# Attention over four images: x of images 1 to 3 loaded in 128-byte pieces and transposed on VectorE, and the halves of a group's output added by an accumulating DMA

## The chip, the cores and the metric

The kernel runs on one core of one Trainium2 chip. A core has five engines, each with its own instruction queue: TensorE (PE: matrix products; PEld is its weight load), VectorE (DVE), ScalarE (ACT), GpSimd (POOL) and SyncE (SP). DMAs are issued from the queues of SP, ACT and POOL and are moved by 16 DMA engines. SBUF is the working memory of 128 partitions, and PSUM the eight banks into which TensorE writes. The metric is device time in microseconds (us) of one execution.

## The reference

x has shape (4, 64, 64, 256): four images of N = 4096 positions with C = 256 channels. The reference computes, for each image,

```python
q = jnp.einsum('bwhc,cd->bwhd', x, Wq) + bq      # 128 channels
k = jnp.einsum('bwhc,cd->bwhd', x, Wk) + bk      # 128 channels
v = jnp.einsum('bwhc,cd->bwhd', x, Wv) + bv      # 256 channels
pq, pk, pv = q.reshape(B, -1, N), k.reshape(B, -1, N), v.reshape(B, -1, N)
energy = jnp.einsum('bcn,bcm->bnm', pq, pk)
attention = jax.nn.softmax(energy, axis=-1)      # 4096 x 4096 for each image
out = jnp.einsum('bcm,bnm->bcn', pv, attention)
return gamma * out.reshape(B, W, H, C) + x
```

All is float32. The reshape does not transpose: it only cuts the same memory into other rows.

## The kernel before, in words

**Precision.** A float32 operand is written as a sum of parts in the faster fp32r type: an upper part h, which ACT makes, and two rests l and d, which DVE makes from h and the operand. A product is then three matmuls. The three parts have the numbers 0, 1 and 2, and part 2 (d) goes into a matmul of its own.

**The main loop.** It runs over n = 0 to 511 (line 693): four images of 128 steps. An image has NG = 8 groups of 512 output columns; a group has NU = 16 steps, t = 0 to 15, and each step takes 256 of the 4096 rows of k. Step n issues, in this order:
- `cross(n + 2)`: the part-2 product of q and k, two matmuls, scaled on ACT (L368, L369);
- `attend(n, 0)`: six matmuls of the exponentials with half of v into the accumulators a0 and b0 (L442);
- `energy(n + 2)`: the other four matmuls of q and k (L383) and two exponentials on ACT (L386);
- `load_k`: a DMA of 384 KB on POOL's queue for step n + 5, into one of three buffers (L355);
- `store()`: stores of finished projections, on SP's queue (L338);
- `upper(n + 2)`: h on ACT (L392);
- `halves(n + 1)` on DVE: the running row sum (L403), l (L418) and d (L420);
- `attend(n, 1)`: six matmuls into a1 and b1;
- `proceed()`: one piece of every group that is being finished.

At t = 15 ACT empties a0 and b0 (L462) into a tile o, in the place of `upper`, and at t = 0 of the next group DVE empties a1 and b1 (L460) into the same tile. The tile o has one buffer, so the first of these waits for the output store of the group before.

**Finishing a group.** `finish` is a generator that advances by one piece with each step. In terms of t of the following group: at t = 15 and 0 the row sums go to DRAM and come back in another layout (zd, two stores; y, eight loads, all on SP's queue); at t = 3 DVE adds the two halves of o (L479); at t = 6 DVE reduces and transposes y and takes the reciprocal (L482 to L490), and SP stores it (L491); at t = 7 SP loads it, spread over all partitions, into a part of the second half of o (L494); at t = 9 DVE multiplies (L497); at t = 10 a DMA on POOL's queue adds x to o in place (L501); at t = 13 SP stores the group's output, 512 KB (L504).

**Projections.** Those of image 0 are made ahead of the loop. Those of images 1 to 3 are made beside the attention of the image before, in `step(p, engine)`: a pair of chunks of x takes R = 16 steps, r = 0 to 15, and from n = 18 on r = t - 1. One group so carries one pair, and images 1 to 3 have 24 pairs. In the order of r:
- r = 0: PE transposes both chunks, eight 128x128 transposes into two PSUM banks (L219);
- r = 1, 2: ACT makes h of each chunk (L155); r = 1 to 4: DVE makes d and l, one operation in each step (L165);
- r = 5, 6: PE multiplies by Wq and Wk (L257), and DVE adds the bias at r = 5 (L285);
- r = 7 to 10: forms of q and k (L307, L310); r = 9 to 12: PE makes v (L274); r = 11 to 14: forms of v;
- r = 12: SP loads the next pair of x, two DMAs of 256 KB (L211), once PE has used up the buffer.

The raw x of a pair and the d of that pair share one buffer (tag "xd", bufs=1).

**The order of the work.** The order on each engine is the order written out here. A scheduler adds the waits: each instruction waits for its inputs and for the release of the buffer that it writes. The DMAs of SP's queue start in order and take eight completion semaphores in turn, and each of them waits until the one eight before it has landed. In image 4 (n from 384 on) there are no projections.

Of the kernel before, what the change touches and what calls it, by code (L numbers as in the profile page):

```python
# [13 lines left out]
ALU = mybir.AluOpType  # L14
# [6 lines left out]
def kernel(  # L21
# [36 lines left out]
    nc = tc.nc  # L58
# [5 lines left out]
    KC = C // P  # L64
# [5 lines left out]
    def columns(t, nb):  # L70
        return t.rearrange("b w h c -> b (w h c)").rearrange(
            "b (a s g f) -> b g a s f", a=P, s=2, f=nb
        )

    XB = 256
    xv = columns(x, XB)
# [24 lines left out]
    with ExitStack() as fast:  # L101
# [43 lines left out]
        qd, kf, vf, units, loads, now = {}, {}, {}, {}, {}, {}  # L145
# [42 lines left out]
        def bank(name, shape, b, ring):  # L188
            if b:
                tile_ = spare(name, shape)  # L190
                now["turn"] += 1
                return tile_
            pool, tag = next(rings[ring])
            return pool.tile(shape, F32, tag=tag, name=name)

        def spare(name, shape):
            pool, tag = now["banks"][now["turn"] % len(now["banks"])]
            return pool.tile(shape, F32, tag=tag, name=name)

        def load_x(b, i):  # L200
            if b == B or i >= NI:
                return
            if b == 0:
                t = xs4[:, i % 4]
                if i:
                    nc.sync.dma_start(t, xv[b, i])
                loads["x", b, i] = t
                return
            pair = work.tile([P, 2, 2, XB], F32, tag="xd", name=f"x_{b}_{i}", bufs=1)
            for u in range(2):  # L210
                nc.sync.dma_start(pair[:, u], xv[b, i + u])  # L211
                loads["x", b, i + u] = pair[:, u]

        def transposed(b, i):
            xs = loads.pop(("x", b, i))
            tp = units["xt", b, i] = bank(f"xt_{b}_{i}", [P, KC, 2, P], b, 0)
            for k in range(KC):
                for s in range(2):
                    nc.tensor.transpose(tp[:, k, s, :], xs[:, s, k * P : (k + 1) * P], ident)  # L219

        def x_forms(b, i):

            y = units.pop(("xt", b, i))
            if b == 0:
                if i % 3 < 2:
                    f = ppool.tile([P, 3, KC, 2, P], F32R, tag="ld", name=f"xf_{b}_{i}")
                else:
                    f = work.tile([P, 4, KC, 2, P], F32R, tag="xf", name=f"xf_{b}_{i}", bufs=1)
                f = [f[:, j] for j in range(3)]
            else:  # L230
                if i % 2 == 0:
                    shape = [P, 2, KC, 2, 2, P]
                    f = work.tile(shape, F32R, tag="xf", name=f"xf_{b}_{i}", bufs=1)
                    d = work.tile([P, *shape[2:]], F32R, tag="xd", name=f"xd_{b}_{i}", bufs=1)
                    now["xf"] = [f[:, 0], f[:, 1], d]
                f = [y_[:, :, i % 2] for y_ in now["xf"]]
            units["xf", b, i] = f
            yield from split(*f, y, b == 0 and i > 1)
# [44 lines left out]
        def seed_qk(b, i):  # L283
            y = units[0, b, i]
            nc.vector.scalar_tensor_tensor(  # L285
                y, y, REST, bias.unsqueeze(1).to_broadcast([P, 2, C]), ALU.mult, ALU.add
            )
# [8 lines left out]
        def seed_v_pair(b, i, eh):  # L296
            y = units["v", b, i, eh]
            nc.scalar.activation(y, y, AF.Identity, bias=bvs[:, eh : eh + 1], scale=REST)
# [45 lines left out]
        def q_tile(g, name, dtype=F32R):  # L344
            return work.tile([P, NJ, 3, P], dtype, tag=f"q{g % 2}", name=name, bufs=1)
# [118 lines left out]
        def finish(n, o, s):  # L464
            b, g = divmod(n, NG)
            r4 = rall[:, n, :]
            for i in range(2):
                nc.sync.dma_start(zd[n, i], s[:, i, :])
            yield
            y = q_tile(n, f"y_{n}", F32).rearrange("p j f a -> p (j f) a")  # L470
            for j in range(NJ):
                for i in range(2):
                    nc.sync.dma_start(
                        y[j * 32 : (j + 1) * 32, NJ * i : NJ * (i + 1)],
                        zd[n, i].rearrange("(a p) (j c) -> j p a c", p=32, j=NJ)[j],
                    )
            for _ in range(3):
                yield
            nc.vector.tensor_tensor(o[:, 0], o[:, 0], o[:, 1], ALU.add)  # L479
            for _ in range(3):  # L480
                yield
            nc.vector.tensor_reduce(  # L482
                y[:, 8].rearrange("p (f c) -> p c f", f=NJ),
                y[:, :8].rearrange("p a (c f) -> p c f a", f=NJ),
                AX.X,
                ALU.add,
            )
            nc.vector.transpose(y[:, 9], y[:, 8])
            nc.vector.tensor_reduce(r4, y[:, 9].rearrange("p (f c) -> p f c", f=NJ), AX.X, ALU.add)
            nc.vector.reciprocal(r4, r4)  # L490
            nc.sync.dma_start(rd[n, :].rearrange("(p j) -> p j", j=NJ), r4)  # L491
            yield
            r = o[:, 1, 0]
            nc.sync.dma_start(r, rd[n, :].partition_broadcast(P))  # L494
            yield
            yield
            nc.vector.tensor_tensor(  # L497
                o[:, 0], o[:, 0], r.unsqueeze(1).to_broadcast([P, 2, NB]), ALU.mult
            )
            yield  # L500
            nc.gpsimd.dma_start(o[:, 0], xg[b, g], accum_op=ALU.add)  # L501
            for _ in range(3):
                yield
            nc.sync.dma_start(og[b, g], o[:, 0])  # L504
# [50 lines left out]
        def step(n, engine):  # L555

            if n < 0:
                return
            b, u = divmod(n, STEPS)
            i, r = divmod(u, R)  # L560
            b, i = b + 1, 2 * i
            if b >= B:
                return
            made = now["made"]

            def begin(key, pieces):
                made[key] = pieces
                next(pieces)

            if engine == "pe":  # L570
                if r == 0:
                    transposed(b, i)
                    transposed(b, i + 1)
                elif r == 5:
                    products(b, i, 0, (2,))
                    products(b, i + 1, 0, (2,))
                elif r == 6:
                    products(b, i, 0, (0, 1))
                    products(b, i + 1, 0, (0, 1))
                elif r in (9, 11):  # L580
                    products_v(b, i, r // 11, (2,))
                elif r in (10, 12):
                    products_v(b, i, r // 12, (0, 1))
            elif engine == "act":
                if r in (1, 2):
                    begin(("x", r - 1), x_forms(b, i + r - 1))
                elif r in (7, 8):
                    begin(("qk", r - 7), qk_forms(b, i + r - 7))
                elif r in (10, 12):
                    seed_v_pair(b, i, r // 12)  # L590
                    if r == 12:
                        load_x(b + (i + 2) // NI, (i + 2) % NI)
                elif r in (11, 13):
                    begin(("v", r // 13), v_pair_forms(b, i, r // 13))
            else:
                if 1 <= r <= 4:
                    next(made["x", (r - 1) // 2])
                elif r == 5:
                    seed_qk(b, i)
                    seed_qk(b, i + 1)  # L600
                elif 7 <= r <= 10:
                    next(made["qk", (r - 7) // 2])
                    if r % 2 == 0:
                        next(made["qk", (r - 7) // 2], None)
                elif 11 <= r <= 14:
                    next(made["v", (r - 11) // 2])
                    if r % 2 == 0:
                        next(made["v", (r - 11) // 2], None)
# [84 lines left out]
        for n in range(B * STEPS):  # L693
            b, u = divmod(n, STEPS)
# [14 lines left out]
            p = n - 2 + (n > 17)  # L709
# [32 lines left out]
            for m in range(2 * NU):  # L742
                c, r = divmod(n + NU - 3 - 13 * m // 16, STEPS)
# [8 lines left out]
    with tc.If(nc.values_load(again[0:1, 0:1]) > 0), ExitStack() as general:  # L752
# [91 lines left out]
        for b in range(B):  # L844
# [16 lines left out]
            for g in range(NG):  # L861
                ps = []
                mx = work.tile([P, 2, NB], F32, tag="mx", name=f"gmx_{b}_{g}")
                for t in range(NP):
# [9 lines left out]
                    p = ppool.tile([P, 2, NB], F32, tag="p", name=f"gp_{b}_{g}_{t}")  # L874
# [6 lines left out]
                tp = ps_t.tile([P, NJ, P], F32, tag="t", name=f"gmt_{b}_{g}")  # L881
# [45 lines left out]
                r = work.tile([P, NB], F32, tag="r", name=f"gr_{b}_{g}")  # L927
# [36 lines left out]
```

## Time and profile before

| | us |
|---|---|
| median of three runs | 2321.32 (2320.11 to 2322.51) |
| the profiled execution | 2319.64 |
| its span, first to last instruction | 2317.9 |
| PE busy | 2307.0 |
| DVE busy | 2174.3 |
| ACT busy | 1796.9 |
| POOL busy | 417.1 |
| granted TensorE clock | 0.999 |

A row of the profile names the line of the kernel, the engine and the operation, then output<-inputs, the shapes, and the count; after a bar the busy time in us and the mean ns of one, and after a second bar the engine's idle time just ahead of these instructions and what ended it. A row of the timeline begins with the start and the duration in us. A row of the waits has the total in us, the count and the longest. A row of DMA issues has the count, the size of one and the median us from issue to landing. Matmuls overlap in the trace, so what PE needs is read from the distance between starts, not from durations.

### The profile page before, as it was taken

Reading aid. Unit: us, or ns where it says so; the run is one execution under the profiler, and the core shown is the slowest. Engines: PE = TensorE matmul, PEld = TensorE weight load, DVE = VectorE, ACT = ScalarE, POOL = GpSimd, SP = SyncE. Lnnn points to the kernel's source line nnn. Section 1 sums busy time; section 2 is a strip of 40 time slices with the busy share of each in tenths; the row PEclk is TensorE's granted clock in tenths of the full one; section 3 lists DMA queues with packets and bytes.
Section 4 is the critical chain, followed back from the end, with each engine's and each line's share of the span. In section 5 each row is a group of like instructions: output and inputs, shape, how many; then the busy total and the mean of one; then the engine's idle time right before and its main releaser. Section 6 shows DMA issues by size and latency. Waiting matters only on the chain.

```text
span 2317.9 us, 31970 instructions
## 1 busy us (share of the span) xinstructions
PE 2307.0 (100%) x10758; PEld 1931.5 (83%) x10758; DVE 2174.3 (94%) x2174; ACT 1796.9 (78%) x2917; POOL 417.1 (18%) x716
## 2 busy tenths in 40 slices
PE   9999999999999999999999999999999999999998
PEld 9888888888888888888888888888888888888887
DVE  8999999999999999999999999999999999888988
ACT  7778777787777777777777777777787777888775
POOL 7111111111221111111122111111112211111110
PEclk9999999999999999999999999999999999999999
DMA  8557765577896776666799667755679855455553
GB/s 273 162 168 207 206 176 154 170 204 205 266 268 184 208 207 179 166 170 194 201 292 267 186 182 207 199 167 165 173 223 289 258 140 141 141 136 149 154 150 97
DMA packets 232190, 445.30 MB, mean 192 GB/s; under 512 B 27986, under 2 KB 109652, under 8 KB 232020
## 3 DMA queue, kind: packets, MB, share of 16 engines
q0 software_dynamic: 101120, 280.54, 45.5%
q1 hardware_dynamic: 130352, 162.38, 20.6%
q8 instruction: 88, 1.44, 0.3%
q14 instruction: 82, 0.67, 0.1%
q10 hardware_dynamic: 548, 0.26, 0.0%
HBM read 321.92 MB, written 120.39 MB: 191 GB/s over the span
## 4 chain that ended last, share of the span: by engine, by line
PE 99%; DVE 0%; ACT 0%; DMA 0%; issue 0%; ACTq 0%; DVEq 0%
PE a L442 40%; PE e L383 20%; PE b L442 20%; PE e L368 10%; PE qv L257 5%; PE v L274 3%; PE xt L219 1%; DMA raw<-in_L_conv_Wk_dram 0%; ACT qv L292 0%; DVE xf L165 0%; PE zp L517 0%; DVE o_last L547 0%; DVE o_last L542 0%; DVE qv L285 0%; DVE o_last L548 0%
## 5 line engine op out<-in xcount | busy, mean ns | idle before, releaser
L386 ACT ACTIVATE x<-e 128x512 f32<-128x512 f32 x960 | 522.4, 596 | 323.6 <-PE e L383 323.5
L369 ACT ACTIVATE e<-e 128x512 f32<-128x512 f32 x1024 | 546.7, 571 | 132.2 <-PE e L368 132.2
L442 PE MATMUL a<-h,v 128*128 128x512 f32 x2048 | 633.5, 390 | 0.0
L442 PE MATMUL a<-ld,v 128*128 128x512 f32 x2048 | 630.9, 389 | 0.0
L442 PE MATMUL b<-ld,v 128*128 128x512 f32 x2048 | 630.8, 389 | 0.0
L418 DVE TENSOR_TENSOR ld<-x,h 128x1024 fp32r<-128x1024 f32 x480 | 584.6, 1218 | 35.1 <-ACT h L392 22.3
L403 DVE TENSOR_TENSOR s<-s,x 128x1024 f32<-128x1024 f32 x480 | 584.2, 1217 | 33.9 <-ACT x L386 32.6
L355 POOL DMA_DIRECT2D k<-kf x512 | 272.5, 532 | 1845.7 <-PE e L383 1745.2
L420 DVE SCALAR_TENSOR_TENSOR ld<-h,x 128x1024 fp32r<-128x1024 f32 x480 | 584.0, 1217 | 0.0
L383 PE MATMUL e<-q,k 128*128 128x512 f32 x2048 | 547.7, 389 | 0.0
L392 ACT ACTIVATE h<-x 128x1024 fp32r<-128x1024 f32 x480 | 510.5, 1064 | 14.3
L442 PEld LDWEIGHTS a<-ld,v 128*128 128x128 f32 x2048 | 384.4, 188 | 80.6
L442 PEld LDWEIGHTS b<-ld,v 128*128 128x128 f32 x2048 | 384.3, 188 | 80.3 <-DVE ld L420 0.2
L383 PEld LDWEIGHTS e<-q,k 128*128 128x128 f32 x2048 | 384.2, 188 | 79.7
L442 PEld LDWEIGHTS a<-h,v 128*128 128x128 f32 x2048 | 379.6, 188 | 74.2
L368 PE MATMUL e<-q,k 128*128 128x512 f32 x1024 | 315.5, 389 | 0.0
L368 PEld LDWEIGHTS e<-q,k 128*128 128x128 f32 x1024 | 191.9, 188 | 39.8
L310 DVE SCALAR_TENSOR_TENSOR f<-f,qv 128x512 fp32r<-128x512 f32 x128 | 85.5, 678 | 0.3
L418 DVE TENSOR_TENSOR ld<-s,h 128x1024 fp32r<-128x1024 f32 x32 | 39.2, 1226 | 46.8 <-ACT h L392 46.8
L257 PE MATMUL qv<-wf,xf 128*128 128x256 f32 x576 | 77.2, 285 | 0.9 <-DVE qv L285 0.4
L257 PEld LDWEIGHTS qv<-wf,xf 128*128 128x128 f32 x576 | 73.7, 191 | 4.1 <-DVE xf L165 0.8
L165 DVE SCALAR_TENSOR_TENSOR vf<-vf,v 128x512 fp32r<-128x512 f32 x96 | 65.2, 679 | 0.0
(88 smaller groups left out, 1126.8 us busy)
## 6 DMA issues: line engine op xcount, KB each, us to landing
k<-kf POOLq DMA_DIRECT2D x512, 384.0 KB, 3.6
vf<-vf SPq DMA_DIRECT2D x96, 384.0 KB, 5.1
v<-vf POOLq DMA_DIRECT2D x96, 384.0 KB, 6.3
kf<-f SPq DMA_DIRECT2D x128, 192.0 KB, 3.7
qd<-f SPq DMA_DIRECT2D x124, 192.0 KB, 3.8
q<-qd POOLq DMA_DIRECT2D x31, 768.0 KB, 6.0
zd<-s SPq DMA_DIRECT2D x62, 256.0 KB, 5.0
y<-zd SPq DMA_DIRECT2D x248, 64.0 KB, 4.4
```

Of the source, the lines that this page charges most:

```text
L257: nc.tensor.matmul(to[:, s, :], left, right.rearrange("p s a -> p (s a)") if w else right, start=(f == 2 and s == k == 0), stop=(f == 1 an ...
L310: nc.vector.scalar_tensor_tensor(f[:, :, :, j, :], h.bitcast(F32), s, y, ALU.mult, op)
L355: nc.gpsimd.dma_start(t, kf[b, u % NU])
L368: nc.tensor.matmul(e, *forms(n, i, 2), start=True, stop=False, skip_group_check=True)
L369: nc.scalar.mul(e, e, -REST)
L383: nc.tensor.matmul(e, *forms(n, i, f), start=False, stop=(f == 1), skip_group_check=True)
L386: nc.scalar.activation(x[:, i, :], e, AF.Exp, scale=(1.0 + E) ** 3 / E)
L392: nc.scalar.activation(h, units[n], AF.Identity, scale=UPPER)
L403: nc.vector.tensor_tensor(s, s, x, ALU.add)
L418: nc.vector.tensor_tensor(l, x, h.bitcast(F32), ALU.subtract)
L420: nc.vector.scalar_tensor_tensor(d, h.bitcast(F32), 1.0 + E, x, ALU.mult, ALU.subtract)
L442: nc.tensor.matmul(to, vall[:, t, i, f, j * P : (j + 1) * P], units[n][f][:, i, :], start=(t == 0 and i == 0 and f != 1), stop=(t == NU - ...
```

## The change

x of a pair is loaded by 16 DMAs instead of two: for each of the two chunks, eight DMAs that each fill 32 partitions and half of the row. Each takes 256 pieces of 128 bytes (32 floats) out of DRAM, so that in SBUF the 32x32 blocks already lie where the transposed matrix has them. What is left is to transpose each 32x32 block in itself, and one DVE instruction per chunk does this, from SBUF to the PSUM bank into which PE wrote before. It runs at r = 1 and r = 2. The first form of each chunk moves on ACT from r = 1, 2 to r = 3, 4, and DVE makes d and l of a chunk in one step, at r = 3 and r = 4. PE has no work at r = 0 any more. Image 0 is loaded and transposed as before.

In `finish`, the addition of the two halves of o at t = 3 is no DVE instruction any more, but a DMA on POOL's queue that adds one half of o onto the other in SBUF. This holds for all 31 groups that `finish` treats.

```diff
             for u in range(2):
-                nc.sync.dma_start(pair[:, u], xv[b, i + u])
-                loads["x", b, i + u] = pair[:, u]
+                raw_x = pair[:, u].rearrange("p s f -> p (s f)")
+                for q in range(4):
+                    for k in range(KC):
+                        nc.sync.dma_start(
+                            raw_x[q * 32 : (q + 1) * 32, k * XB : (k + 1) * XB].rearrange(
+                                "j (s c i) -> j s c i", s=2, c=4
+                            ),
+                            xv[b, i + u].rearrange(
+                                "(c j) s (k q i) -> q k j s c i", j=32, k=KC, q=4
+                            )[q, k],
+                        )
+                loads["x", b, i + u] = raw_x
 
         def transposed(b, i):
             xs = loads.pop(("x", b, i))
             tp = units["xt", b, i] = bank(f"xt_{b}_{i}", [P, KC, 2, P], b, 0)
+            if b:
+                nc.vector.transpose(tp.rearrange("p k s a -> p (k s a)"), xs)
+                return
...
-            nc.vector.tensor_tensor(o[:, 0], o[:, 0], o[:, 1], ALU.add)
+            nc.gpsimd.dma_start(o[:, 0], o[:, 1], accum_op=ALU.add)
...
             if engine == "pe":
-                if r == 0:
-                    transposed(b, i)
-                    transposed(b, i + 1)
-                elif r == 5:
+                if r == 5:
...
             elif engine == "act":
-                if r in (1, 2):
-                    begin(("x", r - 1), x_forms(b, i + r - 1))
+                if r in (3, 4):
+                    begin(("x", r - 3), x_forms(b, i + r - 3))
...
             else:
-                if 1 <= r <= 4:
-                    next(made["x", (r - 1) // 2])
+                if r in (1, 2):
+                    transposed(b, i + r - 1)
+                elif r in (3, 4):
+                    next(made["x", r - 3])
+                    next(made["x", r - 3])
```

## The prediction

> **What bounds the kernel now.** I read the page first (busy shares, then the chain that ended last), then the list of waits, then the timeline of one period in the middle of images 1 to 3.
>
> ```profile
> span 2317.9 us, 31970 instructions
> PE 2307.0 (100%) x10758; PEld 1931.5 (83%) x10758; DVE 2174.3 (94%) x2174; ACT 1796.9 (78%) x2917; POOL 417.1 (18%) x716
> PE 99%; DVE 0%; ACT 0%; DMA 0%; issue 0%; ACTq 0%; DVEq 0%
> ```
> ```profile
> ACT x L386 <- PE e L383: 323.5, 446, 1.4
> PE wp L140 <- DVE ones L132: 1.1, 1, 1.1
> ```
>
> The chain is PE for 99%, and PE's longest wait in the list is 1.1 us at the start; the other engines wait for PE. So whatever PE does less of is gained in full, and whatever makes PE wait is lost in full. What one group costs in PE time is read from where its work begins anew:
>
> ```profile
> 930.69 0.62 PE L442 MATMUL a<-h,v 128*128 128x512 f32 x2
> 932.96 1.03 PE L219 MATMUL xt<-ident,x 128*128 128x128 f32 x8
> 935.66 0.62 PE L442 MATMUL a<-h,v 128*128 128x512 f32 x2
> 939.74 0.62 PE L442 MATMUL a<-h,v 128*128 128x512 f32 x2
> ```
>
> A step without projection work takes 939.74 - 935.66 = 4.08 us, the step with the eight transposes 935.66 - 930.69 = 4.97 us. Eight transposes cost PE 0.89 us.
>
> **Part 1, the transposes leave PE.** 24 pairs x 0.89 us = 21.4 us less. This term is safe: nothing else is in that step.
>
> **Part 2, they go to VectorE, and the addition of the output's halves leaves it.** DVE has 94% of work and no reserve everywhere, so its order matters.
>
> ```profile
> L488 DVE STREAM_TRANSPOSE y<-y 128x128 f32<-128x128 f32 x31 | 9.7, 312 | 1.1
> L509 DVE SCALAR_TENSOR_TENSOR last<-rall,last 128x128 f32<-128x128 f32 x1 | 0.3, 292 | 0.0
> L310 DVE SCALAR_TENSOR_TENSOR f<-f,qv 128x512 fp32r<-128x512 f32 x128 | 85.5, 678 | 0.3
> L479 DVE TENSOR_TENSOR o<-o 128x1024 f32<-128x1024 f32 x31 | 37.7, 1216 | 0.0
> ```
>
> No 128x512 transpose is shown. Below it cannot cost less than the 128x128 one, 0.31 us; above I take four of those, 1.25 us. From 128 to 512 columns another DVE operation grows by 678 - 292 = 386 ns, so I take 312 + 386 = 0.70 us. [...] Where DVE is latest in a period is after the row-sum reduction (L482 and L488):
>
> ```profile
> 951.95 1.21 DVE L403 TENSOR_TENSOR s<-s,x 128x1024 f32<-128x1024 f32 x1
> 953.09 1.21 DVE L418 TENSOR_TENSOR ld<-x,h 128x1024 fp32r<-128x1024 f32 x1
> ...
> 958.57 0.31 DVE L488 STREAM_TRANSPOSE y<-y 128x128 f32<-128x128 f32 x1
> ...
> 961.58 1.22 DVE L420 SCALAR_TENSOR_TENSOR ld<-h,x 128x1024 fp32r<-128x1024 f32 x1
> ```
> ```profile
> 963.97 0.61 PE L442 MATMUL b<-ld,v 128*128 128x512 f32 x2
> ```
>
> L403 lasts 1.21 us and L418 starts 1.14 us after it, so an instruction occupies DVE some 0.07 us less than it lasts: 0.63 us for a transpose, 1.15 us for the removed addition, per group 2 x 0.63 - 1.15 = +0.11 us. L420 makes the last operand of the step, ready at 962.80; PE wants it at 963.97: 1.17 us to spare. The change takes 0.89 us of PE time ahead of it and adds 0.11 us of DVE work, since all that moves (transposes at r = 1, 2, forms bunched at r = 3, 4) lies before this point: 0.2 us remain. So DVE just fits; I add 0.1 us per group, 2.4 us in all, for the times it does not. At 1.25 us per transpose it would be 2 x 0.55 = 1.1 us later, and PE would lose 0.9 us a group; at 0.31 us it would be 0.8 us earlier, which gains nothing, as PE does not wait there.
>
> ```profile
> L155 ACT ACTIVATE xf<-xt 128x512 fp32r<-128x512 f32 x64 | 38.2, 596 | 0.6 <-PE xt L219 0.6
> ```
>
> ACT's two forms move from r = 1, 2 to r = 3, 4: same count, 0.6 us each, in steps where ACT waits for PE anyway (323.5 us above), so they cost nothing. Without that cover they would cost those 0.6 us each.
>
> **Part 3, x arrives in 16 DMAs per pair instead of 2, all on SP's queue, at r = 12.** This is the part I expect trouble from. What SP issues after r = 12:
>
> ```profile
> 911.84 1.20 SPq L211 DMA_DIRECT2D x<-in_x_dram  x2
> 913.14 0.59 SPq L504 DMA_DIRECT2D out_dram<-o  x1
> ...
> 926.66 5.19 SPq L473 DMA_DIRECT2D y<-zd  x8
> ```
>
> The two x loads have 256 pieces of 1 KB each and go out every 0.65 us. A new load has 256 pieces too, of 128 B, so by count of pieces 16 x 0.65 = 10.4 us. The burst of eight y loads, each to 32 partitions as the new ones, gives 5.19 / 8 = 0.65 us as well. So the output store, next in SP's order, starts 10.5 us after the first x load instead of 1.3 us. What waits for this store is the emptying of the accumulators into the one buffer o (bufs=1):
>
> ```profile
> 925.52 0.69 ACT L462 ACTIVATE o<-a,gam 128x512 f32<-128x512 f32 x1
> 926.66 1.10 ACT L369 ACTIVATE e<-e 128x512 f32<-128x512 f32 x2
> 927.64 1.09 ACT L392 ACTIVATE h<-x 128x1024 fp32r<-128x1024 f32 x1
> 927.97 1.07 PE L383 MATMUL e<-q,k 128*128 128x512 f32 x4
> 928.76 1.23 DVE L418 TENSOR_TENSOR ld<-x,h 128x1024 fp32r<-128x1024 f32 x1 [0.32 <-ACT h L392]
> 929.91 1.22 DVE L420 SCALAR_TENSOR_TENSOR ld<-h,x 128x1024 fp32r<-128x1024 f32 x1
> 931.60 0.61 PE L442 MATMUL b<-ld,v 128*128 128x512 f32 x2
> ```
>
> L462 starts 925.52 - 911.84 = 13.68 us after the first x load. Behind it on ACT are the scaling of e, the upper part h, and through h DVE's d, ready at 931.13 for PE's matmul at 931.60: 0.47 us to spare. So PE waits as soon as the store lands later than 13.68 + 0.47 = 14.15 us after the first x load. How long the store takes:
>
> ```profile
> DMA to landing us min/median/max: 3.0/5.2/9.6
> ```
>
> 5.2 us, the median, is with 512 KB of x straight ahead of it; 3.0 us is the minimum, as in image 4, where no x is loaded. With x spread over 10 us I take 4.0 us, between the two (the ends of this term are in rivals A and B): 10.5 + 4.0 = 14.5 us, 0.35 us of PE wait. 22 groups have both an x load and a store. In six of them the queues are fuller: four fall into the loading of the next image's v, and two more have a store that lands late, as the one at 1057 us (7.1 us, first row). Of the four, the stretch from 622 to 640 us against a common one:
>
> ```profile
> out_dram<-o SPq DMA_DIRECT2D x1, 512.0 KB, 7.1
> ```
> ```profile
> 622.00:640.00 18.00, 18.00 (x81) 14.92 (x80) 15.47 (x18) 14.57 (x26) 4.24 (x8) 1.00 1.11 378
> 912.00:930.00 18.00, 18.00 (x81) 14.89 (x80) 15.16 (x17) 15.00 (x26) 2.31 (x5) 1.00 0.83 250
> ```
> ```profile
> x<-in_x_dram SPq DMA_DIRECT2D x2, 256.0 KB, 7.9
> out_dram<-o SPq DMA_DIRECT2D x1, 512.0 KB, 9.6
> ```
>
> (The windows' last two columns are DMA share and GB/s, 1.11 and 378 against 0.83 and 250; the landings are of 622 to 640 us.) SP's DMAs take eight completion semaphores in turn, so the ninth x load waits until the first has landed. At 7.9 us that makes 7.9 + 8 x 0.65 = 13.1 us of burst, and with a store of 9.6 us a wait of 8.6 us; with no hold-up and 5 us it is 1.4 us. I take 3.5 us. Sum of part 3: 16 x 0.35 + 6 x 3.5 = 5.6 + 21 = 26.6 us. Behind the store SP's vf, zd and y follow some 9 us later; y is read by the reduction that runs just before L488's 958.57, and y's last issue would move from 926.66 + 5.19 = 931.85 to some 940 at worst, so 10 us are left and this costs nothing; without them DVE would stand, and PE after it. x itself was read by PE at 932.96 and is read by DVE a step later, near 937; it lands near 911.84 + 10.4 + 4 = 926.
>
> **Part 4, the accumulating DMA on POOL's queue.** One of this kind already runs in each group:
>
> ```profile
> L501 POOL DMA_DIRECT2D o<-in_x_dram x31 | 34.9, 1124 | 1.2 <-ACT h L392 1.1
> ```
> ```profile
> o<-in_x_dram POOLq DMA_DIRECT2D x31, 512.0 KB, 6.7
> ```
> ```profile
> 942.80 1.22 DVE L479 TENSOR_TENSOR o<-o 128x1024 f32<-128x1024 f32 x1
> ```
> ```profile
> 960.89 0.34 SPq L494 DMA_DIRECT2D o<-rd  x1
> ```
>
> 31 x 1.12 us = 35 us more of POOL, which is 18% busy. It is issued where the addition stood (942.80) and lands 6.7 us later, near 950; the first that needs it is SP's load of r into the freed half at 960.89. So 11 us are left, and I cost it at nothing. If that cover were gone, the r load would wait on SP, and DVE's product by r after it. Behind it on POOL's queue are the k loads, as they are behind the one that already runs, and PE shows no wait for k; if a k load came late, PE would lose what it is late by. In image 4 it frees DVE, and PE sets the pace there: no gain.
>
> **The sum.** -21.4 + 2.4 + 26.6 = +7.6 us on the profiled execution's 2319.64 us, so 2327. That execution lies 1.7 us under the median of the three runs, 2321.32, so I predict 2329 us. 0.2% is 4.6 us, about what a measurement of this kernel can tell from no change.
>
> **The rivals.**
> *A, the burst stays hidden (faster).* The point that decides is 14.15 us from the first x load to the store's landing. With the store's minimum of 3.0 us and 0.65 us per load it lands at 13.5, and only the full queues cost, 6 x 1.4 = 8 us: 2321.3 - 21.4 + 8 = 2308; with nothing at all 2300. For it: the margin is missed by only 0.35 us in my sum. Against it: six groups with fuller queues, and every load that takes over 0.68 us to issue.
> *B, small pieces land slowly (much slower).* If a new load lands in 6.5 us instead of under 5.2, the eight semaphores make the burst 16 x 6.5 / 8 = 13 us, the store lands at 17.1, and 22 x 2.95 = 65 us go: 2365. At the 7.9 us of the full stretch, everywhere, 15.8 us of burst and 22 x 5.65 = 124 us: 2424. For it: those 7.9 us. Against it: a load carries 32 KB, and y loads of 64 KB average 0.65 us apart. [...]
> *C, VectorE becomes the bound.* At 1.25 us per transpose PE loses 0.9 us in 24 groups, 22 us, on top of part 3: 2321.3 - 21.4 + 26.6 + 22 = 2348. For it: only 0.2 us to spare. Against it: the slope of the other DVE operations.
>
> **How the numbers follow.** My forecast, a small loss from the late store (2315 to 2345): 0.47, of which 0.35 slower, 0.10 same, 0.02 faster. A: 0.30 (0.28 faster, 0.02 same). B: 0.15, C: 0.08, slower. Together faster 0.30, same 0.12, slower 0.58. The range leaves out the lowest of A and the upper half of B: 2301 to 2375. The forecast's own range is 2315 to 2345.
>
> **What would show it.** A group of images 1 to 3 gets 0.89 us shorter, plus its waits. L462 on ACT has an idle gap ended by the output store's DMA (right) or none (A). PE has waits at L383 or L442, once per group, for ACT's e or DVE's ld. The x burst on SP takes 10.4 us; 13 or more means B. The transpose's mean is 0.70 us; near 1.2 means C. I am wrong altogether if PE waits somewhere else, for k or for x.

## The result, and the profile after

The changed kernel takes 2340.24 us (median, 2335.46 to 2345.00) against 2321.27 us of the kernel before: a ratio of 1.008, 95% interval 1.0067 to 1.0094. It is slower by 0.8%, where the prediction had 2329 us. The profiled execution took 2337.3 us with a span of 2335.5 us, against 2319.64 and 2317.9 us before. Lines from L219 on are 13 higher than before: L442 is now L455, L462 is L475, L460 is L473, L420 is L433, L504 is L517, L479 is L492. The x loads are L214, and VectorE's transpose is L228.

The page first (span, busy times, shares of the chain), then three rows of the list of waits:

```profile
span 2335.5 us, 32160 instructions
PE 2299.6 (98%) x10566; PEld 1914.1 (82%) x10566; DVE 2163.8 (93%) x2191; ACT 1797.0 (77%) x2917; POOL 445.0 (19%) x747
PE 83%; SPq 8%; DMA 5%; issue 1%; DVE 1%; ACT 1%; ACTq 0%; DVEq 0%
```
```profile
PEld a L455 <- ACT o L475: 32.6, 22, 5.5
ACT o L475 <- DMA out_dram<-o: 32.2, 22, 5.4
PE a L455 <- ACT o L475: 23.2, 20, 5.0
```

PE is busy 7.4 us less than before (2307.0 to 2299.6), and yet the span is 17.6 us longer. The chain was PE for 99%; now SP's queue (8%) and DMAs (5%) stand in it. The waits name the place: 22 times, once for each group that has both an x load and an output store, ACT's emptying of the accumulators waits for the output store to land, and PE's next matmul into these accumulators waits for ACT. Before, no wait of PE was longer than 1.1 us, and none was of this kind.

One common group, from the timeline (start, duration, engine, line; the bracket is the idle time just before):

```profile
919.69 10.49 SPq L214 DMA_DIRECT2D x<-in_x_dram  x16
...
926.29 0.62 PE L455 MATMUL a<-h,v 128*128 128x512 f32 x2
...
930.28 0.59 SPq L517 DMA_DIRECT2D out_dram<-o  x1
930.37 0.62 PE L455 MATMUL a<-h,v 128*128 128x512 f32 x2
...
934.32 0.69 ACT L475 ACTIVATE o<-a,gam 128x512 f32<-128x512 f32 x1 [0.85 <-DMA out_dram<-o]
...
935.06 0.73 PE L455 MATMUL a<-h,v 128*128 128x512 f32 x2 [0.45 <-ACT o L475]
...
939.27 0.62 PE L455 MATMUL a<-h,v 128*128 128x512 f32 x2
```

The 16 loads occupy SP's queue for 10.49 us, the store starts 10.59 us after the first of them, and L475 starts 14.63 us after it, having waited 0.85 us. PE's wait is seen in the distance between the steps' first matmuls: 930.37 - 926.29 = 4.08 us undisturbed, 935.06 - 930.37 = 4.69 us with the wait, and 939.27 - 935.06 = 4.21 us for the step behind it. Before, the store started 1.3 us after the first x load.

The output store, the x loads and the new transposes by line (the first two rows are the median time from issue to landing, in the last column; then the transposes' mean of 718 ns and no idle time before them):

```profile
out_dram<-o SPq DMA_DIRECT2D x31, 512.0 KB, 3.7
x<-in_x_dram SPq DMA_DIRECT2D x384, 32.0 KB, 2.8
L228 DVE STREAM_TRANSPOSE xt<-x 128x512 f32<-128x512 f32 x48 | 34.5, 718 | 0.0
```

The longest waits fall into the stretches in which v of the next image is loaded. One of them, in the timeline and then in windows (us, busy times with counts of PE, PEld, DVE, ACT, POOL, then the granted TensorE clock, DMA share and GB/s):

```profile
643.15 0.69 ACT L475 ACTIVATE o<-a,gam 128x512 f32<-128x512 f32 x1 [5.11 <-DMA out_dram<-o]
...
643.89 1.22 PE L455 MATMUL a<-h,v 128*128 128x512 f32 x2 [4.71 <-ACT o L475]
```
```profile
639.30:643.20 3.90, 0.00 (x0) 0.00 (x0) 0.03 (x1) 0.05 (x1) 0.00 (x0) 1.00 0.99 314
643.30:650.00 6.70, 6.11 (x14) 4.79 (x15) 5.58 (x6) 5.06 (x8) 1.18 (x3) 0.50 0.92 343
650.10:655.00 4.90, 4.90 (x23) 4.04 (x22) 3.55 (x4) 3.19 (x6) 1.36 (x3) 1.00 1.06 302
```

PE stands still for 4.71 us, and then the clock granted to it is 0.50 for 6.8 us: a pair of matmuls that takes 0.62 us elsewhere is listed with 1.22 us. The prediction had no such term.

### The profile page after: what moved, and what is told of

It reads as the page before. It is cut to its first block, busy times and chain, and to the rows that moved or that the text cites. A ratio compares the mean times of both kernels' runs of the same rounds, so it can differ in the third digit from the quotient of the medians.

```text
span 2335.5 us, 32160 instructions
## 1 busy us (share of the span) xinstructions
PE 2299.6 (98%) x10566; PEld 1914.1 (82%) x10566; DVE 2163.8 (93%) x2191; ACT 1797.0 (77%) x2917; POOL 445.0 (19%) x747
## 4 chain that ended last, share of the span: by engine, by line
PE 83%; SPq 8%; DMA 5%; issue 1%; DVE 1%; ACT 1%; ACTq 0%; DVEq 0%
PE a L455 34%; PE e L396 17%; PE b L455 17%; PE e L381 8%; SPq L214 8%; PE qv L270 5%; DMA out_dram<-o 4%; PE v L287 2%; DMA x<-in_x_dram 1%; ACT o L475 1%; DMA qd<-f 0%; DVE s L416 0%; DVE ld L433 0%; PE xt L232 0%; DMA rows<-in_L_conv_bk_dram 0%
## 5 line engine op out<-in xcount | busy, mean ns | idle before, releaser
L455 PE MATMUL a<-h,v 128*128 128x512 f32 x2048 | 635.8, 392 | 23.4 <-ACT o L475 23.2
L455 PE MATMUL a<-ld,v 128*128 128x512 f32 x2048 | 632.9, 390 | 0.0
L455 PE MATMUL b<-ld,v 128*128 128x512 f32 x2048 | 632.4, 390 | 0.1
L433 DVE SCALAR_TENSOR_TENSOR ld<-h,x 128x1024 fp32r<-128x1024 f32 x480 | 584.2, 1217 | 0.0
L455 PEld LDWEIGHTS a<-h,v 128*128 128x128 f32 x2048 | 380.6, 188 | 107.4 <-ACT o L475 32.6
L455 PEld LDWEIGHTS b<-ld,v 128*128 128x128 f32 x2048 | 384.9, 188 | 82.1 <-DVE ld L433 1.4
L455 PEld LDWEIGHTS a<-ld,v 128*128 128x128 f32 x2048 | 385.6, 188 | 81.2
L270 PEld LDWEIGHTS qv<-wf,xf 128*128 128x128 f32 x576 | 73.7, 191 | 3.5 <-issue 0.8
```

The lines of the kernel that those rows point to most:

```text
L270: nc.tensor.matmul(to[:, s, :], left, right.rearrange("p s a -> p (s a)") if w else right, start=(f == 2 and s == k == 0), stop=(f == 1 an ...
L433: nc.vector.scalar_tensor_tensor(d, h.bitcast(F32), 1.0 + E, x, ALU.mult, ALU.subtract)
L455: nc.tensor.matmul(to, vall[:, t, i, f, j * P : (j + 1) * P], units[n][f][:, i, :], start=(t == 0 and i == 0 and f != 1), stop=(t == NU - ...
```

## The experiments

All diffs are against the changed kernel, unless the text says otherwise. Ratios are to the kernel before.

### The output store ahead of the x loads

The store is issued one step earlier, at t = 12, and so leaves SP before the burst.

```diff
             nc.gpsimd.dma_start(o[:, 0], xg[b, g], accum_op=ALU.add)
-            for _ in range(3):
+            for _ in range(2):
                 yield
             nc.sync.dma_start(og[b, g], o[:, 0])
```

> The changed kernel with the output store one step earlier, so that SP issues it ahead of the 16 x loads; nothing else differs. Theory (the store behind the x burst makes L475, and through it PE, wait): the store lands long before L475 wants it, the rows of waits on out_dram<-o go away, PE loses none of the 36.75 us that groups 1 to 23 of the changed kernel lost over 70.92 us each, nor the two stretches at half clock: 2340.2 - 37 = some 2303 us, 0.8% faster than before, and a common group takes 70.9 to 71.0 us. Rival 1 (the small pieces themselves, or DVE's transposes, cost the time, and the late store only takes the blame): the groups stay above 71.5 us and the time near 2340 us. Rival 2 (the store ahead delays x in its turn): the store row goes away and a wait for x takes its place, 2310 to 2330 us.

Measured: 2300.69 us (2300.57 to 2303.79), ratio 0.9913, interval 0.9896 to 0.9929: faster than both kernels. From its page (shares of the chain) and the timeline of the same group:

```profile
PE 99%; DVE 0%; DMA 0%; ACT 0%; ACTq 0%; issue 0%; DVEq 0%
```
```profile
904.59 0.60 SPq L517 DMA_DIRECT2D out_dram<-o  x1
...
905.51 10.98 SPq L214 DMA_DIRECT2D x<-in_x_dram  x16
...
916.20 0.62 PE L455 MATMUL a<-h,v 128*128 128x512 f32 x2
...
919.18 0.69 ACT L475 ACTIVATE o<-a,gam 128x512 f32<-128x512 f32 x1
...
920.28 0.62 PE L455 MATMUL a<-h,v 128*128 128x512 f32 x2
```

The burst is as long as it was (10.98 us), with the same pieces, transposes and accumulating DMA. L475 has no wait, it starts at 13.67 us after the first x load as in the kernel before (13.68), and the step is 920.28 - 916.20 = 4.08 us. Every group from the third on takes 70.92 us to within 0.03, where it was 71.81 us before. No stretch at half clock is left between the first matmuls and the last. So the order on SP's queue costs all that the changed kernel loses to its waits; from the third group on, the small pieces, VectorE's transposes and the accumulating DMA cost PE nothing. In the first two groups VectorE is late, here as in the changed kernel; this row of the waits stands against one wait of 0.2 us before:

```profile
PEld b L442 <- DVE ld L420: 0.2, 1, 0.2
```
```profile
PEld b L455 <- DVE ld L433: 1.4, 4, 0.5
```

Besides the one of before, two waits lie in the first group (at t = 5 and 7) and one in the second (at t = 8); they lengthen these groups by 0.7 and 0.25 us. In the first group VectorE gets the two transposes, and there is no addition yet that could leave it, since `finish` first adds in the second group.

### The accumulating DMA alone

Here the diff is against the kernel before.

```diff
-            nc.vector.tensor_tensor(o[:, 0], o[:, 0], o[:, 1], ALU.add)
+            nc.gpsimd.dma_start(o[:, 0], o[:, 1], accum_op=ALU.add)
```

> The kernel before with the accumulating DMA alone in place of DVE's addition; x is loaded and transposed as before. Theory (the accumulation costs nothing and, DVE not being the bound there, gains nothing): 2321 us, within 0.1% of before. Rival (an accumulating DMA of 512 KB on POOL's queue holds up k or r): 2325 us or more, with a wait of PE for k or of DVE for r.

Measured: 2321.04 us (2320.87 to 2322.18), ratio 1.0004, interval 0.9994 to 1.0013: no change. The row of its DMA on the page, and the busy times:

```profile
o<-o POOLq DMA_DIRECT2D x31, 512.0 KB, 5.3
```
```profile
PE 2307.9 (99%) x10758; PEld 1932.2 (83%) x10758; DVE 2149.8 (93%) x2143; ACT 1796.5 (77%) x2917; POOL 445.3 (19%) x747
```

DVE does 24.5 us less (2174.3 to 2149.8), and nothing comes of it, since PE sets the pace. One small thing is common to all six kernels with this DMA: from the first matmul of the last group to the end of the span they take 73.7 us, against 72.5 us in the three without it. PE's steps in the last group are those of before, and the last store is issued 6.5 us after the last step's first matmul in both; the 1.2 us lie behind it, at the end of the program. What makes it up was not tried.

### VectorE's addition restored

The accumulating DMA is taken out again, x stays as changed.

```diff
-            nc.gpsimd.dma_start(o[:, 0], o[:, 1], accum_op=ALU.add)
+            nc.vector.tensor_tensor(o[:, 0], o[:, 0], o[:, 1], ALU.add)
```

> The changed kernel with DVE's addition of the output's halves restored in place of the accumulating DMA; x stays in 128-byte pieces, transposed by DVE. Theory (DVE has 0.40 us to spare at its last operand, b L455, in the changed kernel, and the addition takes 1.15 us of it): DVE is late by 0.75 us in each of 23 groups less what PE has already waited in that group (0.5 to 0.75 us in common groups), so between 2340 and 2357 us, with a row of PE waiting at L455 for DVE's ld. Rival (the accumulating DMA, as the new traffic on the queues, is what delays the store): the store lands earlier and the time falls below 2335 us.

Measured: 2354.81 us (2350.53 to 2359.52), ratio 1.0140, interval 1.0123 to 1.0157. From its waits:

```profile
ACT o L475 <- DMA out_dram<-o: 33.3, 22, 5.3
PE a L455 <- ACT o L475: 24.5, 22, 4.9
PEld b L455 <- DVE ld L433: 22.9, 46, 0.8
PE b L455 <- DVE ld L433: 8.0, 20, 0.4
```

The waits for the store are there as before, so the accumulating DMA did not delay it; and a new wait has come, of PE for VectorE's last operand. The group's loss over 70.92 us has a median of 1.86 us against 0.79 in the changed kernel. By PE's steps the two losses add: 38.0 us lie at the waits for the store and in the two steps behind them (36.5 us in the changed kernel), and 20.5 us at t = 6 and t = 8, where PE waits for VectorE.

### The store ahead, and VectorE's addition restored

Both edits together.

> Both edits: the output store ahead of the x loads, and DVE's addition restored. What x in small pieces and DVE's transposes are worth when the store is out of the way and the accumulating DMA is not there. Theory: 2303 us of the kernel with the store ahead + 23 x (1.15 - 0.40 = 0.75) = 17 us of PE waiting for DVE's ld at L455: 2320 us, so the accumulating DMA is what makes room for the transposes. Rival (DVE catches up elsewhere, since its addition is not on the way to L455): 2303 us.

Measured: 2318.55 us (2316.99 to 2319.58), ratio 0.9991, interval 0.9981 to 1.0001. Its waits and one place in the timeline:

```profile
PEld b L455 <- DVE ld L433: 20.4, 27, 0.8
PE b L455 <- DVE ld L433: 9.0, 23, 0.4
```
```profile
961.78 1.22 DVE L433 SCALAR_TENSOR_TENSOR ld<-h,x 128x1024 fp32r<-128x1024 f32 x1
...
963.05 0.73 PE L455 MATMUL b<-ld,v 128*128 128x512 f32 x2 [0.40 <-DVE ld L433]
```

The store's wait is gone and VectorE's alone is left, nearly all of it at t = 8, once in each group: L433 ends at 963.00 and PE's matmul starts at 963.05. From the third group on, the groups take 71.67 to 71.71 us instead of 70.92, 23 x 0.77 = 17.7 us, about the difference of the medians to the kernel with the store ahead, 2318.55 - 2300.69 = 17.9 us. So the transposes on VectorE are worth some 19 us (2319.97 us before in these runs, less 2300.69), but only where the addition has left it; with both on VectorE the gain is all but given back.

### The same loads in pieces of 1 KB

```diff
-                            raw_x[q * 32 : (q + 1) * 32, k * XB : (k + 1) * XB].rearrange(
-                                "j (s c i) -> j s c i", s=2, c=4
-                            ),
-                            xv[b, i + u].rearrange(
-                                "(c j) s (k q i) -> q k j s c i", j=32, k=KC, q=4
-                            )[q, k],
+                            raw_x[q * 32 : (q + 1) * 32, k * XB : (k + 1) * XB],
+                            xv[b, i + u][q * 32 : (q + 1) * 32, k],
```

> The changed kernel, its 16 x loads of 32 KB each in 32 pieces of 1 KB in place of 256 of 128 B. x lies then not in the order that the transposes need, so the values of images 1 to 3 are others; count, sizes and order of all else stay. Theory (a load's issue takes time by its pieces): 32 pieces take about the 0.34 us of the short loads on SP, 16 x 0.34 = 5.5 us of burst, the store lands about 9.5 us after the first load, ahead of L475's 13.68, no waits, no half clock: about 2302 us. Rival 1 (issue takes 0.65 us per DMA whatever its pieces, so that their number alone counts): burst 10.4 us and 2340 us as in the changed kernel. Rival 2 (the small pieces' slow landing, not their issue, delays the store): burst 10.4 us, but the store lands at 13.5 us or before and the time falls to 2310 to 2325 us.

Measured: 2307.09 us (2306.30 to 2309.60), ratio 0.9946, interval 0.9929 to 0.9962. From its timeline, the group that starts at 905 us, and its waits:

```profile
905.13 7.68 SPq L214 DMA_DIRECT2D x<-in_x_dram  x16
912.90 0.55 SPq L513 DMA_DIRECT2D out_dram<-o  x1
...
918.80 0.69 ACT L471 ACTIVATE o<-a,gam 128x512 f32<-128x512 f32 x1
```
```profile
ACT o L471 <- DMA out_dram<-o: 6.3, 4, 2.3
```

(L471 is the emptying, L475 in the changed kernel.) The burst is 7.7 us, neither the 5.5 us of the theory nor the 10.4 us of the first rival. So a load costs SP 7.68 / 16 = 0.48 us with 32 pieces and 10.49 / 16 = 0.66 us with 256: most of it comes with the DMA, and only 0.18 us with the smaller and more numerous pieces. Their number rather than their size makes these 0.18 us: the two loads of before, of 256 pieces of 1 KB each, held SP for 913.14 - 911.84 = 1.30 us, 0.65 us each. The shorter burst is enough here: the store starts 7.8 us after the first load and not 10.6, no common group waits, and four waits are left in the crowded stretches. A load lands in a median of 2.6 us, against 2.8 us with 128-byte pieces, so it is not the landing of small pieces that delays the store.

### 24 and 32 loads for a pair

Every second load, and then every load, is cut in two; pieces and bytes stay. The core of the second:

```diff
-                        nc.sync.dma_start(
-                            raw_x[q * 32 : (q + 1) * 32, k * XB : (k + 1) * XB].rearrange(
...
+                        for s in range(2):
+                            at = k * XB + s * P
+                            nc.sync.dma_start(
+                                raw_x[q * 32 : (q + 1) * 32, at : at + P].rearrange(
+                                    "j (c i) -> j c i", c=4
+                                ),
+                                xv[b, i + u].rearrange(
+                                    "(c j) s (k q i) -> q k s j c i", j=32, k=KC, q=4
+                                )[q, k, s],
+                            )
```

> The changed kernel with every second x load cut in two, 24 loads a pair, pieces still of 128 B and as many. If issue time goes by pieces alone, the burst stays 10.4 us and the time 2340 us. If a load has a fixed part, too (0.34 us for the shortest loads on SP against 0.61 for 256 pieces, so some 0.46 us for 128), the burst is 8 x 0.61 + 16 x 0.46 = 12.2 us, the store lands 1.8 us later and PE loses 22 x 1.8 = 40 us more: 2380 us. If waits of about 2 to 3 us each are enough for the granted clock to halve as it did after the two longest waits of the changed kernel, 22 x 1.7 (one stretch of 3.4 us at half speed) to 22 x 3.4 come on top: 2420 to 2455 us; if only waits of 4.7 us and more do so, no more than a handful of such stretches.

> The changed kernel with every x load cut in two, 32 loads a pair, pieces of 128 B as before. By pieces alone: 2340 us. With a fixed part, 32 x 0.46 = 14.7 us of burst, the store lands 4.3 us later, PE waits some 5 us in each of 22 groups: 2340 + 22 x 4.3 = 2435 us with the clock held, and with the half clock after each such wait, as after the two of 4.7 and 5.0 us in the changed kernel (about 3 us each), 2435 + 20 x 3 = 2495 us, with about 22 stretches of half clock in the profile.

Measured, one execution each: 2463.64 us with 24 loads, 2480.31 us with 32. The median burst is 14.5 and 16.0 us, against 10.7 us with 16 loads. Waits of the first (24 loads), and windows around one of them:

```profile
ACT o L487 <- DMA out_dram<-o: 109.4, 22, 6.2
PE a L467 <- ACT o L487: 100.6, 22, 5.8
```
```profile
287.40:289.70 2.30, 0.00 (x0) 0.00 (x0) 0.00 (x0) 0.00 (x0) 0.00 (x0) 1.00 0.94 286
289.90:296.50 6.60, 4.71 (x11) 3.75 (x12) 4.75 (x5) 3.84 (x7) 0.00 (x0) 0.50 0.91 349
296.70:300.00 3.30, 3.30 (x16) 2.74 (x15) 2.91 (x3) 2.49 (x4) 0.53 (x1) 1.00 0.75 208
```

More DMAs with the same bytes and pieces make a later store, as the theory has it. The 24 loads cost more than was expected (14.5 us of burst instead of 12.2, and 2463.64 us, above every time that was named). Within a burst the starts lie 0.63 us apart behind a load of 256 pieces, and 0.64 and 0.47 us behind the two loads of 128 that follow it (medians), 8 x 1.74 = 13.9 us before any hold-up; with 32 loads, all of 128 pieces, it is 0.47 us throughout, as for the loads of 32 pieces (0.46). So the issue time is no straight line in the number of pieces, and the first load behind one of 256 pieces costs as much as that one; why was not tried. Each of the 22 waits of 4.1 to 5.8 us is followed by a stretch at half clock. In the steps where the wait lies, PE loses 104 us, and in the steps behind them, where the clock is half, 57 us. With 32 loads it is 127 and 53 us. There, too, each of the 22 waits is followed by half clock, so the 2435 us of "the clock held" are excluded.

## Why the prediction was right, and where it was off

Sign and mechanism held: a small loss, from the output store that SP issues behind the x burst. The size did not: 7.6 us were forecast and 17.7 came. Two terms that the prediction did not have, the steps behind the waits and the half clock, make up 9.6 of the 10.1 us that are missing. That the long waits came out 4.8 us lower and the common ones 5.1 us higher, so that the two nearly cancel, is luck. The steps in turn, against the profiled execution:

| step | predicted, us | measured, us |
|---|---|---|
| transposes leave PE | -21.4 | -21.4 |
| VectorE late | +2.4 | +0.9 |
| waits for the store, five long ones (predicted: six) | +21.0 | +16.2 |
| waits for the store, 17 common ones (predicted: 16) | +5.6 | +10.7 |
| the two steps behind each wait | 0 | +3.6 |
| half clock after two waits | 0 | +6.0 |
| accumulating DMA | 0 | +1.2 |
| start of the first group | 0 | +0.5 |
| sum | +7.6 | +17.7 |

The first two measured rows come from the kernel with the store ahead: from the first matmul into the accumulators of the first group to that of the 25th it takes 1703.1 us, against 1723.6 before, which is 20.5 us less; 24 steps are 0.89 us shorter, and VectorE's waits in the first two groups take 0.9 us back. The others are from the steps of the changed kernel, and the sum agrees with the spans' 2335.5 - 2317.9 = 17.6 us. The start of the first group is not the change's doing: over the nine kernels it lies anywhere from 64.8 to 68.3 us after the span's start.

**The transposes leave PE.** Right in price: the step that held them takes 4.08 us instead of 4.97 in each of the 24 groups, 0.89 us less. The first group as a whole gained only 0.2 us and the second 0.65, for VectorE's waits.

**VectorE.** 0.70 us per transpose was taken and 718 ns measured, so rival C had no ground. The reserve at t = 8, predicted as 0.2 us, is 0.39 us:

```profile
970.10 1.22 DVE L433 SCALAR_TENSOR_TENSOR ld<-h,x 128x1024 fp32r<-128x1024 f32 x1
971.71 0.62 PE L455 MATMUL b<-ld,v 128*128 128x512 f32 x2
```

The prediction added 0.1 us per group for the times when it would not do. It did from the third group on. Of the 0.9 us of the first two, 0.7 come from what the prediction passed over, that the first group has no addition to take away; what delays VectorE in the second group was not looked into. The restored addition (1.15 us) showed that this reserve is the real limit: it cost 0.77 us per group. By size, 312 ns at 128 columns and 718 ns at 512 are 406 / 384 = 1.06 ns for each further column, where the 386 ns that the prediction took from another operation are 1.01 ns. Four times the small one, 1.25 us, is excluded.

**The burst and the store.** 16 loads at 0.65 us, 10.4 us: measured 10.4 to 11.3 us in common groups, and the store starts after 10.8 us in the median instead of 10.5. (One of the two sources of the 0.65 us did not hold: of the seven distances between the starts of the eight y loads, five are 0.47 to 0.52 us, and one of 1.64 us, a hold-up, lifts the mean to 0.65.) The store was given 4.0 us; its median is 3.7 over all groups and 3.6 in common ones. The two errors cancel by luck, and the store lands 14.5 us after the first x load in the median of the common groups whose landing is recorded, as predicted.

What was mis-sized is the reserve. The threshold was put at 14.15 us from the first x load, by ACT's later work and VectorE's d. In fact PE meets the wait earlier and more directly: its next matmul needs the accumulator itself, which L475 has to empty first. Before, L462 (a) ended at 925.52 + 0.69 = 926.21, and the next first matmul into a followed here:

```profile
926.61 0.62 PE L442 MATMUL a<-h,v 128*128 128x512 f32 x2
```

That is 0.40 us, not 0.47, and 0.05 us of it pass between ACT's end and PE's start (935.01 and 935.06 in the common group above). So PE waits when L475 starts later than 13.68 + 0.35 = 14.03 us after the first x load. In each of the 17 common groups the start of L475 less PE's loss in that step is 14.02 or 14.03 us. L475 also starts some 0.1 us after the store's landing, so the threshold for the landing is 13.9 us instead of 14.15, and the common wait is 0.63 us in the mean instead of 0.35. Between a wait and none there were only a few tenths of a us, so that each tenth was worth 2 us in the sum.

**The crowded stretches.** Six waits of 3.5 us were predicted. Five are long: 4.9, 2.0, 1.9, 5.2 and 2.3 us of PE's step. Four lie beside v's loading, as expected. The fifth (2.3 us) lies in a group whose store took 5.1 us before and 5.7 us now; the two groups that were counted for a late store (7.1 and 7.0 us before) lost 0.2 and 0.6 us. The hold-up through the eight semaphores shows as a burst of 12.6 to 13.3 us in the four groups beside v's loading, where 13.1 had been worked out, but the store there took 3.0 to 5.9 us to land, not 9.6.

**The clock.** No term stood for it. The two waits of 4.7 and 5.0 us were each followed by 6.8 us at a granted clock of 0.50, which cost 3.0 us each. The experiment with 24 loads repeats it 22 times.

**The accumulating DMA.** Costed at nothing; it lands in 5.3 us and takes no one's place: alone, it gave a ratio of 1.0004. The kernels that have it take 1.2 us more at the end of the program, and it is what makes room on VectorE.

**The rivals.** A (the burst hidden) did not happen here, by a few tenths of a us per group, and is what the kernel with the store ahead does: 2300.7 us, where the prediction had "with nothing at all 2300". B's mechanism, a slow landing of small pieces, is refuted: 2.8 us median against 6.5 or more, and with pieces of 1 KB the landing takes 2.6 us, only 0.2 us less. What the pieces do cost is SP's time to issue them: 16 x 0.18 = 2.9 us more of burst with 256 pieces a load than with 32.

## What to carry to other kernels

A DMA that is cut into many does not only move bytes: it holds the queue that issues it, here for 0.48 us with 32 pieces and 0.66 us with 256, and what stands behind it in program order starts later, here the store of a common group 10.8 us (median) after the first load instead of 1.3. Before such a burst is put ahead of a store whose buffer is wanted again, look for the reserve of that buffer in the timeline, and issue the store first; here one step decided between 0.8% slower and 0.9% faster. Moving work from the bounding engine to one that is 94% busy pays only up to that engine's reserve at its latest point (0.39 us here, and the restored addition of 1.15 us cost 0.77 us per group), so what it gives up in exchange belongs to the same change.

## What was not expected of the hardware

In these runs the granted TensorE clock fell to half (0.50) after some pauses of PE, in stretches of 3.41 us or a multiple (3.41, 6.83 and 10.24 us in the runs with 24 and 32 loads), which began 2.0 to 4.6 us after PE stopped. In the changed kernel, pauses of 4.71 and 5.04 us were each followed by one, pauses of up to 2.17 us by none. With 24 loads, 22 pauses of 4.1 to 5.8 us were followed by 22 stretches. In the kernel with VectorE's addition restored, a pause of 1.85 us was followed by a stretch of 3.41 us, while two of 1.74 and 1.75 us were not. So the length of a pause alone did not decide: 2.17 us passed, 1.85 us did not.

What sets the two apart can be read from the traces. Within one run the stretches begin on a grid: any two starts lie a whole number of times 3.4133 us apart, to within 0.004 us (22 starts with 24 loads, 22 with 32). In the changed kernel they are 643.22 and 1298.58, 192 x 3.4133 us apart. Cut into intervals of this grid, the pause of 2.17 us falls apart into 0.33 and 1.84 us, while the pause of 1.85 us lies in one interval whole. First come the second interval of the pause of 2.17 us (changed kernel) and the one behind it; then the interval of the pause of 1.85 us (VectorE's addition restored), the one at half clock behind it, and the next. PE's busy time stands behind the length of 3.41 us, the granted clock third from the end:

```profile
1373.67:1377.08 3.41, 1.57 (x7) 1.31 (x8) 2.29 (x3) 2.31 (x5) 0.00 (x0) 1.00 1.04 308
1377.08:1380.49 3.41, 3.41 (x17) 2.81 (x16) 2.73 (x4) 3.38 (x6) 0.53 (x1) 1.00 0.87 309
```
```profile
1235.87:1239.28 3.41, 1.56 (x8) 0.98 (x7) 1.13 (x3) 1.16 (x3) 0.93 (x2) 1.00 1.09 304
1239.28:1242.69 3.41, 3.41 (x9) 2.63 (x10) 2.75 (x3) 2.29 (x4) 0.00 (x0) 0.50 1.05 310
1242.69:1246.10 3.41, 3.41 (x17) 2.80 (x16) 3.41 (x4) 3.14 (x5) 1.59 (x3) 1.00 1.04 406
```

The same holds from the first step to the last in all runs: of the intervals at full clock, each of the 49 in which PE stood idle for 1.85 us or more was followed by one at half clock, and none with 1.84 us or less was. An interval at half clock was followed by another when PE was idle in it for 0.59 us or more, and by full clock at 0.53 us or less; this makes the stretches of 6.83 and 10.24 us. The ends of matmuls are modelled in the trace, so these limits may be off by some hundredths of a us.

In these kernels, then, a pause that was to be harmless wherever it fell had to stay under some 1.8 us: 1.85 us of idle in one interval were followed by half clock.
